# One sum in the output instead of two, a branch at the end of the program and quarter tiles at a later place, in a gated cross-attention and mixture-of-experts kernel

## The chip, the cores and the metric

The kernel runs on one core of a Trainium2 chip. The metric is the device time of one execution in microseconds (us), as the median of several runs; less is better. The engines are PE (TensorE: matmuls and the loads of their weights), DVE (VectorE), ACT (ScalarE), POOL (GpSimd) and SP (SyncE, which here only issues DMAs). Each engine takes its own instructions in order and waits for the others by semaphores.

## The reference

Eight sequences of 256 tokens with 256 features go through a gated cross-attention to 120 context rows (16 heads of 64) and then through a gated mixture of eight experts, two for each token. Cut to what matters:

```python
x = x + tanh(g_xattn) * xattn(layernorm(x), ctx)       # out @ w_out + b_out at its end
def ffn(x, W1, W2, Wr):                                # x: (2048, 256); W1: (8, 1024, 256)
    probs = softmax(einsum('btd,ed->bte', x, Wr))
    vals, idx = top_k(probs, 2)
    gate = sum over the two of  vals / vals.sum(-1) * one_hot(idx, 8)
    h = silu(einsum('btd,efd->btef', x, W1))
    y = einsum('btef,edf->bted', h, W2)
    return einsum('bte,bted->btd', gate, y)
x = x + tanh(g_ffn) * ffn(layernorm(x), W1, W2, Wr)
```

All values are float32.

## The kernel before

**Attention.** A loop over 32 units (sequence, half of the heads, half of the tokens) does the attention. As soon as a sequence is through, its x is the first part of the result; the routing works out each token's two experts, and 32 indirect DMAs of POOL (L366) send each token's normalised row, with its eight gate values and its token number, into the list of each of its experts. The lists lie in a DRAM tensor `routed`. Slots that no token fills hold zeros and a number from 2048 upwards.

**Experts.** The second loop walks a written list `order` of 31 tiles of 128 rows: eight "first" tiles (the first 128 rows of each expert) and the "full" tiles 8 to 30, whose expert is known only at run time. Full tiles 0 to 7 (`SPARE`) and four of the six quads exist for distributions that need more tiles. A "quad" is a tile of four quarters of 32 rows, from up to four experts, for what is left of the lists; two quads (`MIXED`) are worked in halves between the full tiles, so that a quad spreads over four tiles of the list. In iteration i of this loop:

- `go_up` (L837): 32 matmuls with w1 for tile i, then Silu on ACT
- `open_tile`: for tile i+1, DVE copies its expert's w1 (L808) and gate (L813), PE turns its rows (L828), DVE copies them back (L830)
- DVE copies w2 of tile i (L817)
- `close_tile`: 16 matmuls with w2 for tile i-1 (L853), DVE scales the result by the gate into `y` (L861), and `add_up` adds the rows of y to their tokens' rows with an indirect DMA of POOL (L879)
- SP loads the rows of tile i+4 (L796), into one of six buffers (`xt`); the two quads' rows, which POOL gathers (L784), share these buffers

A quad has, in the same iterations, its copies of weights on ACT (L926), its matmuls (L944, L965) and four adds of 32 rows each. There are two buffers for `y`.

**The order of the sums.** Each add waits for the landing of the one before (`last_add`), since two may hit one token's row. There are two places for the sums. The DRAM tensor `acc` has 2048 rows for tokens and 128 more, into which unused slots are added. x is first written into `acc`. The first tiles, the quads and the full tiles 8 to 15 add into `acc`. Then SP copies `acc` to the output `out` (L900), and the last 15 full tiles (`SURE`), which have no unused slots in any case, add into `out`.

**The branch.** Before iteration `always` = 16 a `tc.If(more > 0)` (L1153 in the profile) holds the work of the spare full tiles and of quads 2 to 5. The value `more` is loaded into a register of every engine four iterations earlier. For these inputs it is zero: the branch is passed on all engines, but each has to test it, jump over the body, and bring the semaphores that the body would have raised up to their values. The two quads are mixed into the eight iterations ahead of it.

**Who sets the order.** PE, DVE, ACT and SP keep the order in which the program is written; POOL's instructions are placed by the scheduler. SP is in order too: a load that is written behind the copy of L900 is issued behind it.

Of the kernel before, what the change touches and what calls it, by code (L numbers as in the profile page):

```python
# [9 lines left out]
F32 = mybir.dt.float32  # L10
# [5 lines left out]
P = 128  # L16
# [4 lines left out]
E, DFF = 8, 1024  # L21
# [15 lines left out]
EARLY = 2  # L37
QUARTER = 32
FULLS = 31
SURE = 15  # L40
SPARE = 8
QUADS = 6
MIXED = 2
# [6 lines left out]
def tile_gated_xattn_moe(  # L50
# [36 lines left out]


    routed = tc.dram_tile([E * T + P, XW], F32, name="routed")


    acc = tc.dram_tile([T + P, D], F32, name="acc")

# [295 lines left out]
    ctxT_sb = ap.tile([P, DC, B * M], F32, name="ctxT_sb", bufs=1)  # L391

    x_v = x.rearrange("(n p) d -> p n d", p=P)
    acc_v = acc[:T, :].rearrange("(n p) d -> p n d", p=P)
    ctx_v = ctxT.rearrange("(c p) t -> p c t", p=P)
    wkv_v = w_kv.rearrange("(c p) f -> p c f", p=P)
    wq_v = w_q.rearrange("(c p) f -> p c f", p=P)
# [42 lines left out]
            empty.unsqueeze(1).to_broadcast([P, NBLK, XW]),  # L440
        )
    nc.sync.dma_start(routed[ds(NOWHERE, P), :], empty)
    nc.sync.dma_start(acc[ds(T, P), :], empty[:, :D])

    xns = {}
    norms_x = norms_y = None
# [147 lines left out]
    def norm_y(b, k):  # L594
        nonlocal norms_y
        g = b // 2
        if k == 0:
            if b % 2 == 0:
                groups[g] = [], late.tile([P, DC, GT], F32, tag="xn2T", name=f"xn2T_{g}")
            groups[g][0].append(  # L600
                late.tile([P, 2, XW], F32, tag="rows", name=f"rows_{b}", bufs=4)
            )
            norms_y = Norms(2, f"y{b}")
        norms_y.add(xs[b][:, k, :], groups[g][0][-1][:, k, :D])
        if k == 1:
            nc.sync.dma_start(acc_v[:, ts(b, 2), :], xs[b])
            norms_y.root()

    def turn_y(b, bank):
# [162 lines left out]
    def load(t):  # L772
        kind, i = t
        xt = take(fp, [P, XW], "xt", f"xt_{kind}{i}", bufs=6)
        if kind == "first":
            first = nc.sync.dma_start(xt, routed[ds(i * T, P), :])
            for send in behind:
                tc.declare_no_dep(
                    first.ins, send.ins, reason="rows behind those of the first tiles"
                )  # L780
            firsts.append(first)
            return xt
        if kind == "quad":
            nc.gpsimd.indirect_dma_start(  # L784
                out=xt,
                out_offset=None,
                in_=routed[:, :],
                in_offset=bass.IndirectOffsetOnAxis(
                    ap=tables[1][0][:, i : i + 1], axis=0
                ),  # L790
            )
            return xt
        start = nc.sync.value_load(
            tables[0][1][0:1, i : i + 1], min_val=0, max_val=NOWHERE
        )
        nc.sync.dma_start(xt, routed[ds(start, P), :])  # L796
        return xt
# [52 lines left out]
    def down(t, hT, gate, xt, w2):  # L850
        py = take(fw[2], [P, 512], "mm", f"py_{t[0]}{t[1]}")
        for f in range(FC):
            nc.tensor.matmul(  # L853
                py[:, :D],
                lhsT=hT[:, f, :],
                rhs=w2[:, f, :],
                start=(f == 0),
                stop=(f == FC - 1),
            )
        y = take(fw[3], [P, D], "y", f"y_{t[0]}{t[1]}")  # L860
        nc.vector.tensor_scalar(y, py[:, :D], gate, None, ALU.mult)  # L861
        add_up(t, y, xt)

    def add_up(t, y, xt, parts=1):


        sure = t[0] == "full" and t[1] >= FULLS - SURE
        slots = xt[:, XID : XID + 1].bitcast(I32)
        if parts > 1:

            slots = take(fw[3], [P // parts, parts], "slots", f"slots_{t[1]}", dtype=I32)
            for k in range(parts):
                nc.vector.tensor_copy(
                    slots[:, k : k + 1],
                    xt[ts(k, P // parts), XID : XID + 1].bitcast(I32),
                )
        for k in range(parts):
            own = ts(k, P // parts)
            add = nc.gpsimd.indirect_dma_start(  # L879
                out=out[:, :] if sure else acc[:, :],  # L880
                out_offset=bass.IndirectOffsetOnAxis(
                    ap=slots[:, k : k + 1], axis=0
                ),
                in_=y[own, :],
                in_offset=None,
                compute_op=ALU.add,
            )

            if last_add:
                tc.add_manual_dep(  # L890
                    add.ins,
                    last_add[-1].ins.name,
                    mybir.DependencyInfo(
                        mybir.DependencyClass.Sync, mybir.DependencyReason.DATA
                    ),
                    reason="sums of one token",
                )
            last_add.append(add)
        if t == ("full", FULLS - SURE - 1):
            move = nc.sync.dma_start(out, acc[:T, :])  # L900
            last_add.append(move)


    octets = {}
# [87 lines left out]
    def close_tile():  # L992
        if state["pending"] is not None:
            down(*state["pending"])
            state["pending"] = None
# [5 lines left out]

    order = [("first", e) for e in (0, 1, 2, 6, 3, 4, 5, 7)]
    order += [("full", j) for j in range(SPARE, FULLS)]
    always = E + FULLS - SURE - SPARE
    AHEAD = 4
    xts = {}

# [140 lines left out]
    load_expert(5)  # L1148
    g = NG - 1
    for i, t in enumerate(order):  # L1150
        if i == always:

            with tc.If(more > 0):  # L1153
                spare = {}
                for j in range(SPARE):
                    tj = ("full", j)
                    xt = load(tj)
                    w1, gate, copy_w2 = weights(tj, xt)
                    w2 = copy_w2()
                    down(tj, up(tj, turn(tj, xt), w1), gate, xt, w2)  # L1160
                for j in range(MIXED, QUADS):
                    for _ in quad(j, load(("quad", j))):
                        pass
                spare = None
        if i == always - 4:
            more = nc.values_load(tables[1][3][0:1, 0:1], min_val=0, max_val=FULLS)
        w2_of = state["ready"][2][2]
        if i == 2:
            turn_y(B - 1, bank_tr)


        if i == always - 4 * MIXED - 1:
            quads = [quad(j, xt) for j, xt in enumerate(quad_xts)]
        mixed = i in range(always - 4 * MIXED, always)
        if mixed and i % 4 == 0:
            running = quads[(i - always) // 4 + MIXED]
        if mixed and i != always - 4 * MIXED:
            next(running)
        new = go_up()
        if i == always - 4 * MIXED - 1:  # L1180
            next(quads[0])
        copies = []
        if i == 1:
            for k in range(2):
                copies.append(wide_out(B - 1, k, ps_py))
        if i == 2:
            lg = logits(g, groups[g][1], bank_tr)
            next(lg)
        for k, copy in enumerate(copies):
            copy()  # L1190
            norm_y(B - 1, k)
        if i + 1 < len(order):
            open_tile(order[i + 1], xts[i + 1])
        if mixed:
            next(running)
        if i == 0:
            norms_y.finish()
            weigh(B - 1, 1, ps_py)
            load_expert(4)
            turn_y(B - 2, bank_tr)  # L1200
            sending[g - 1] = places(g - 1, groups[g - 1][0], picked[g - 1], bank_tr)
        if i == 3:
            sending[g] = places(g, groups[g][0], picked[g], bank_tr)
        w2 = w2_of()
        close_tile()
        state["pending"] = *new, w2
        if mixed:
            next(running)
        if i == 1:
            norms_y.finish()  # L1210
        if i == 2:
            lg = next(lg)
            picked[g] = router(g, lg)
        if i < 2:
            for _ in range(2):
                next(sending[g - 1])
        if 2 < i < 5:
            for _ in range(2):
                next(sending[g])
        if i == 4:  # L1220
            parts = table()
            routing_pool.close()
            qp.append(
                ctx.enter_context(
                    tc.tile_pool(name="quads", bufs=1, side="right", reuse_waits="tile")
                )
            )
        if 3 < i < 6:
            tables.append(next(parts))
        while len(xts) <= min(i + AHEAD, len(order) - 1 if tables else 7):  # L1230
            xts[len(xts)] = load(order[len(xts)])
        if i == 5:
            quad_xts = [load(("quad", j)) for j in range(MIXED)]
        if i == 1:
            load_expert(3)
            load_expert(7)
    close_tile()


# [41 lines left out]
```

## Time and profile before

| | |
|---|---|
| median of 3 runs | 556.06 us (555.69 to 557.33) |
| the profiled execution's own time | 555.92 us |
| its span in the profile | 553.8 us |
| PE busy in the span | 529.6 us (96%) |
| weight loads of PE | 448.8 us (81%) |
| DVE, ACT, POOL busy | 285.7, 219.8, 128.3 us |
| mean granted clock of PE | 0.988 |

The span begins with the first instruction and ends with the last; 2.1 us of the execution's time lie outside. A matmul overlaps the next one's weight load, and where PE is busy without gaps it sets the time; the other engines matter where PE, or the last add, waits for them. [...]

### The profile page before, as it was taken

How to read it: one execution, taken by the hardware profiler on the slowest of the kernel's cores; microseconds unless marked ns; L12 is line 12 of the kernel's file. 1: busy time of each engine (PE TensorE's matmuls, PEld its weight loads, DVE VectorE, ACT ScalarE, POOL GpSimd, SP SyncE). 2: the span in 40 equal slices, each digit the busy share in tenths (PEclk: the TensorE clock that was granted, in tenths of full speed). 3: DMA queues.
4: the chain of work that ended last, by engine and by line, in shares of the span. 5: the costliest groups of instructions: out<-in, count | busy, mean ns of one | idle time of the engine just before them, and what ended most of it. 6: DMA issues, size and time to landing. Idle time of an engine off the chain costs nothing. (4 is left out here: it accounts for less than half of the span.)

```text
span 553.8 us, 10097 instructions
## 1 busy us (share of the span) xinstructions
PE 529.6 (96%) x3796; PEld 448.8 (81%) x3796; DVE 285.7 (52%) x683; ACT 219.8 (40%) x700; POOL 128.3 (23%) x135
## 2 busy tenths in 40 slices
PE   7999999999999999999999999999997959999992
PEld 7788878878788787887788989878786959999992
DVE  3676555568655686455742474445343423444430
ACT  1666464564655645556521204455460100111110
POOL 2021100100331003200024463122433423211222
PEclk9999999999999999999999999999999989999997
DMA  8999970500705001020299632222031053222111
GB/s 298 334 308 294 309 219 18 171 22 1 225 35 181 22 1 60 31 69 1 97 381 306 181 89 40 39 30 43 8 51 36 9 181 60 39 40 40 20 19 19
DMA packets 46630, 59.88 MB, mean 108 GB/s; under 512 B 3088, under 2 KB 41616, under 8 KB 46544
## 3 DMA queue, kind: packets, MB, share of 16 engines
q1 hardware_dynamic: 39680, 49.58, 29.3%
q0 software_dynamic: 6480, 8.94, 9.2%
q8 instruction: 32, 0.52, 0.4%
q10 hardware_dynamic: 416, 0.66, 0.4%
q14 instruction: 22, 0.18, 0.1%
HBM read 30.77 MB, written 30.50 MB: 111 GB/s over the span
## 5 line engine op out<-in xcount | busy, mean ns | idle before, releaser
L539 ACT ACTIVATE pr<-psc,mx 128x120 f32<-128x120 f32 x256 | 88.4, 372 | 65.3 <-DVE mx L533 55.9
L837 PEld LDWEIGHTS ph_full<-xT_full,w 128*128 128x128 f32 x736 | 85.2, 192 | 9.2 <-issue 8.5
L837 PE MATMUL ph_full<-xT_full,w 128*128 128x128 f32 x736 | 87.0, 276 | 3.2 <-PEq L1153 2.3
L853 PE MATMUL py_full<-w,hT_full 128*128 128x256 f32 x368 | 84.9, 385 | 0.0
L853 PEld LDWEIGHTS py_full<-w,hT_full 128*128 128x128 f32 x368 | 69.6, 194 | 8.9
L845 ACT ACTIVATE hT_full<-ph_full 128x1024 f32<-128x1024 f32 x23 | 23.5, 1023 | 108.6 <-PE ph_full L837 108.6
L489 PE MATMUL pq<-xnT,w_sb 128*128 128x256 f32 x256 | 62.7, 388 | 0.4 <-DVE xnT L208 0.4
L583 PE MATMUL pw<-w_sb 128*128 128x256 f32 x256 | 58.6, 382 | 0.0
L527 DVE TENSOR_REDUCE mx<-psc 128x8 f32<-128x960 f32 x32 | 37.0, 1156 | 37.5 <-PE psc L519 37.3
L539 ACT ACTIVATION_READ_ACCUMULATOR pr<-psc,mx 128x1 f32 x256 | 55.6, 217 | 0.0
L489 PEld LDWEIGHTS pq<-xnT,w_sb 128*128 128x128 f32 x256 | 46.6, 190 | 10.8 <-issue 3.1
L583 PEld LDWEIGHTS pw<-w_sb 128*128 128x128 f32 x256 | 47.4, 190 | 8.7 <-issue 2.5
L366 POOL DMA_INDIRECT routed<-rows,slot x32 | 31.8, 995 | 56.4 <-DVE slot L362 49.4
L879 POOL DMA_INDIRECT out_dram<-y_full,xt_full x15 | 25.4, 1693 | 77.6 <-DVE y_full L861 57.6
L559 ACT COPY w_sb<-tr 120x512 f32<-120x512 f32 x64 | 34.6, 597 | 19.3 <-PE tr L558 19.3
L548 DVE TENSOR_TENSOR pr<-pr,sm 128x960 f32<-128x960 f32 x32 | 37.1, 1158 | 1.1
L861 DVE TENSOR_SCALAR y_full<-py_full,gate 128x256 f32<-128x256 f32 x23 | 11.1, 484 | 51.1 <-PE py_full L853 44.7
L519 PE MATMUL psc<-kT,w_sb 64*128 64x120 f32 x512 | 37.2, 284 | 0.0
L926 ACT COPY part<-w_sb 128x1024 f32 x32 | 31.1, 1043 | 14.8 <-PE py_q L965 14.2
L519 PEld LDWEIGHTS psc<-kT,w_sb 64*128 64x128 f32 x512 | 31.1, 187 | 6.4 <-issue 3.6
L558 PEld LDWEIGHTS tr<-ident,pr 128*120 128x120 f32 x256 | 29.5, 138 | 5.9 <-issue 4.3
L558 PE MATMUL tr<-ident,pr 128*120 128x128 f32 x256 | 33.5, 273 | 0.1
(175 smaller groups left out, 685.0 us busy)
## 6 DMA issues: line engine op xcount, KB each, us to landing
routed<-w_sb SPq DMA_DIRECT2D x8, 2120.0 KB
w_sb<-in_w1T_dram SPq DMA_DIRECT2D x8, 1024.0 KB
w_sb<-in_w2T_dram SPq DMA_DIRECT2D x8, 1024.0 KB
xt_full<-routed SPq DMA_DIRECT2D x23, 132.5 KB
acc<-x SPq DMA_DIRECT2D x8, 256.0 KB
x<-in_x_dram SPq DMA_DIRECT2D x7, 256.0 KB
w_sb<-in_w_kv_dram SPq DMA_DIRECT2D x3, 512.0 KB
xt_first<-routed SPq DMA_DIRECT2D x8, 132.5 KB
```

Source lines behind the costliest of these rows:

```text
L366: send = nc.gpsimd.indirect_dma_start(out=routed[:, :], out_offset=bass.IndirectOffsetOnAxis(ap=slot[:, i : i + 1], axis=0), in_=rows[h][: ...
L489: nc.tensor.matmul(pq[:, i, :], lhsT=wq_sb[:, c, ts(2 * h + i, P)], rhs=xnT[:, c, :], start=(c == 0), stop=(c == DC - 1),)
L519: nc.tensor.matmul(psc[:, j, ts(i, M)], lhsT=qT[ts(j, DH), 4 * o + i, ts(nb, P)], rhs=kT[ts(j, DH), 4 * o + i, :], start=True, stop=True,)
L527: nc.vector.tensor_reduce(mx.rearrange("p (j i) -> p j i", i=4), psc[:, :, : 4 * M].rearrange("p j (i m) -> p j i m", m=M), AX.X, ALU.max,)
L539: nc.scalar.activation(pr[:, h, :], psc[:, j, ts(i, M)], AF.Exp, bias=mx[:, h : h + 1], scale=QK_SCALE, accum_out=sm[:, h : h + 1],)
L548: nc.vector.tensor_tensor(pr, pr, sm.unsqueeze(2).to_broadcast([P, 8, M]), ALU.mult)
L558: nc.tensor.transpose(tr[:M, i, :], pr[:, 4 * j + i, :], ident)
L559: nc.scalar.copy(pT_sb[:, ts(j, 4), ts(nb, P)], tr[:M, :, :])
L583: nc.tensor.matmul(pw[:, :D], lhsT=oT_sb[b % 2][:, ci, ts(k, P)], rhs=wo_sb[:, ci, :], start=(ci == 0), stop=(ci == IC - 1),)
L837: nc.tensor.matmul(ph[:, f, :], lhsT=w1[:, c, ts(f, P)], rhs=xT[:, c, :], start=(c == 0), stop=(c == DC - 1),)
L853: nc.tensor.matmul(py[:, :D], lhsT=hT[:, f, :], rhs=w2[:, f, :], start=(f == 0), stop=(f == FC - 1),)
L926: nc.scalar.copy(w[:, q, :].rearrange("p (a b) -> p a b", b=D if down else DFF // 2), slab[:, ts(h, FC // 2), :] if down else slab[:, :, t ...
```

## The change

- `acc` is gone. x is written into `out`, and every add goes into `out`. The add gets a bound, the last token's number: a slot with a higher number is left out of the DMA (so the 128 spare rows, their filling, the constant `SURE` and the copy of L900 go too).
- The branch with the spare tiles, and the load of `more`, stand behind the last `close_tile`.
- The two quads are mixed into iterations 16 to 23 instead of 8 to 15. Their gathers are written in iteration 12 instead of 5, and their first copies of weights in iteration 15 instead of 7.

```diff
-SURE = 15
...
-    acc = tc.dram_tile([T + P, D], F32, name="acc")
...
-    acc_v = acc[:T, :].rearrange("(n p) d -> p n d", p=P)
+    out_v = out.rearrange("(n p) d -> p n d", p=P)
...
-    nc.sync.dma_start(acc[ds(T, P), :], empty[:, :D])
...
-            nc.sync.dma_start(acc_v[:, ts(b, 2), :], xs[b])
+            nc.sync.dma_start(out_v[:, ts(b, 2), :], xs[b])
...
-        sure = t[0] == "full" and t[1] >= FULLS - SURE
...
             add = nc.gpsimd.indirect_dma_start(
-                out=out[:, :] if sure else acc[:, :],
+                out=out[:, :],
                 out_offset=bass.IndirectOffsetOnAxis(
                     ap=slots[:, k : k + 1], axis=0
                 ),
                 in_=y[own, :],
                 in_offset=None,
                 compute_op=ALU.add,
+                bounds_check=T - 1,
+                oob_is_err=False,
             )
...
-        if t == ("full", FULLS - SURE - 1):
-            move = nc.sync.dma_start(out, acc[:T, :])
-            last_add.append(move)
...
-    always = E + FULLS - SURE - SPARE
+    mix = 16
...
-        if i == always:
-            with tc.If(more > 0):
-                ...
-        if i == always - 4:
-            more = nc.values_load(tables[1][3][0:1, 0:1], min_val=0, max_val=FULLS)
...
-        if i == always - 4 * MIXED - 1:
+        mixed = mix <= i < mix + 4 * MIXED
+        if i == mix - 1:
             quads = [quad(j, xt) for j, xt in enumerate(quad_xts)]
-        mixed = i in range(always - 4 * MIXED, always)
         if mixed and i % 4 == 0:
-            running = quads[(i - always) // 4 + MIXED]
-        if mixed and i != always - 4 * MIXED:
+            running = quads[(i - mix) // 4]
+        if mixed and i > mix:
             next(running)
         new = go_up()
-        if i == always - 4 * MIXED - 1:
+        if i == mix - 1:
             next(quads[0])
...
-        if i == 5:
+        if i == mix - 4:
             quad_xts = [load(("quad", j)) for j in range(MIXED)]
...
     close_tile()
+
+    more = nc.values_load(tables[1][3][0:1, 0:1], min_val=0, max_val=FULLS)
+    with tc.If(more > 0):
+        spare = {}
+        for j in range(SPARE):
+            tj = ("full", j)
+            xt = load(tj)
+            w1, gate, copy_w2 = weights(tj, xt)
+            w2 = copy_w2()
+            down(tj, up(tj, turn(tj, xt), w1), gate, xt, w2)
+        for j in range(MIXED, QUADS):
+            for _ in quad(j, load(("quad", j))):
+                pass
+        spare = None
```

More of the change, by code (lines that the diff above doesn't have):

```diff
@@ L1150, in tile_gated_xattn_moe @@
     for i, t in enumerate(order):
-        if i == always:
[L1153 to L1164, printed above, removed]
-        if i == always - 4:
-            more = nc.values_load(tables[1][3][0:1, 0:1], min_val=0, max_val=FULLS)
         w2_of = state["ready"][2][2]
```

## The prediction

> **What bounds the kernel now.** I read first the row of busy time and the forty slices of the page: TensorE (PE) is busy for 529.6 of 553.8 us, and its digits fall below 9 almost only near the end. So what PE idles is what can be won. Then I asked for a table by stage of the last part (columns: length, busy time and count of PE, weight load, DVE, ACT, POOL, then granted TensorE clock, DMA share, GB/s):
>
> ```profile
> 339.00:420.00 81.00, 80.89 (x638) 65.41 (x636) 34.79 (x61) 41.54 (x45) 22.05 (x14) 1.00 0.21 34
> 420.00:450.00 30.00, 25.81 (x182) 24.22 (x182) 12.09 (x21) 4.04 (x4) 10.35 (x6) 1.00 0.25 55
> 450.00:462.00 12.00, 7.28 (x32) 6.38 (x33) 2.85 (x5) 0.06 (x1) 3.72 (x2) 0.72 0.44 132
> 462.00:544.00 82.00, 81.55 (x552) 76.24 (x550) 34.94 (x53) 11.27 (x11) 20.14 (x12) 1.00 0.24 35
> 544.00:554.00 10.00, 0.00 (x0) 0.00 (x0) 0.07 (x1) 0.00 (x0) 1.54 (x1) 0.68 0.12 15
> ```
>
> PE is full while the eight mixed tiles run (339 to 420) and in the plain tiles from 462 on. It loses time at 420 to 462, there also with a granted clock of 0.72, and 10 us pass behind its last matmul. The timeline of PE over those holes:
>
> ```profile
> 417.96 1.93 PE L965 MATMUL py_q<-part,hqT 128*32 128x256 f32 x32
> 422.15 2.25 PE L837 MATMUL ph_full<-xT_full,w 128*128 128x128 f32 x18 [2.25 <-PEq L1153]
> 425.38 1.83 PE L837 MATMUL ph_full<-xT_full,w 128*128 128x128 f32 x14 [0.98 <-issue]
> ...
> 434.29 0.38 PE L828 MATMUL xtT_full<-ident,xt_full 128*128 128x128 f32 x2
> ...
> 437.96 3.73 PE L837 MATMUL ph_full<-xT_full,w 128*128 128x128 f32 x32
> ...
> 454.72 0.66 PE L828 MATMUL xtT_full<-ident,xt_full 128*128 128x128 f32 x2 [5.78 <-DMA xt_full<-routed]
> 455.18 5.44 PE L853 MATMUL py_full<-w,hT_full 128*128 128x256 f32 x16
> 460.45 3.73 PE L837 MATMUL ph_full<-xT_full,w 128*128 128x128 f32 x32
> ```
>
> The first hole stands where the branch is (L1153): 2.25 us before the next tile's matmuls, 0.98 us in the middle of them. The second waits for the DMA of a tile's rows. Why was that DMA late? The waits of the DMA queues say it (total us, times, longest):
>
> ```profile
> SPq L900 <- DMA acc<-y_full,xt_full: 21.9, 1, 21.9
> ```
>
> The records of the branch's line, and of the program's last line, give prices used below (minimum/median/maximum ns, first and last start):
>
> ```profile
> L1153 PEldq COMPARE_BRANCH x1: 3542/3542/3542, 418.4 to 418.4; - x1
> ...
> L1153 POOLq COMPARE_BRANCH x1: 53/53/53, 435.8 to 435.8; - x1
> L1153 POOLq INC_SWDGE_SEM x1: 1324/1324/1324, 439.0 to 439.0; - x1
> ```
>
> ```profile
> L1277 POOLq DRAIN x3: 46/113/7812, 545.2 to 553.5; - x3
> ```
>
> And POOL's timeline around the branch:
>
> ```profile
> 418.83 1.54 POOL L879 DMA_INDIRECT acc<-y_full,xt_full  x1 [7.05 <-DVE y_full L861]
> 423.42 1.32 POOL L879 DMA_INDIRECT acc<-half,slots  x1 [3.04 <-DMA acc<-y_full,xt_full]
> ...
> 435.40 2.05 POOL L879 DMA_INDIRECT acc<-half,slots  x1 [2.36 <-DVE xT_full L830]
> 441.19 2.74 POOL L879 DMA_INDIRECT acc<-y_full,xt_full  x1 [3.73 <-DVE y_full L861]
> ```
>
> SP stands 21.9 us at L900, the copy of acc into out, until the last add into acc has landed; tile loads are queued behind it. That add is late because four quarter adds stand before it, each waiting for its predecessor's landing: the chain from 418.83 to 441.19.
>
> **The change part by part.** *The move of acc goes.* No DMA of L900, no 21.9 us wait on SP, no pair of 2 MB streams. The next load, issued at 447.85, is no longer behind it. PE gets back its 5.78 us of idle, and the slow stretch after it: 454.72 to 460.45 is 5.73 us, where the same three groups take 437.96 - 434.29 = 3.67 us, so 2.06 us more. Together **-7.84 us**. Late next is that load's own condition, a free row buffer. Two of the six are held by the quarters; the others come free when an add has landed. For the tile that waits longest (the first one loaded from the buffer of a tile four earlier, with a plain tile between) I take a plain tile's own times: add issued 8.2 us after its tile's up starts, landed 3.7 us later, load about 2.1 us, so the rows are there at 14 us and are turned at 2 x 7.24 + 3.6 = 18.1 us. Some 4 us are left: nothing.
>
> *The branch leaves the middle.* PE gets back 2.25 + 0.98 = **-3.23 us**. DVE's 1.1 us there was under PE's. Without this hole PE comes 3.2 us closer to the add chain. The four quarter adds and the next add follow at 4.0 us on average; DVE's y two tiles later must wait for the add of the tile before (two y buffers). Worked from the rows: that y could start 22.1 us after the quad's last matmul and its add buffer is free at 24.4, so DVE is held 2.3 us. Behind it on DVE stand the copy of w1 (1.23 us), the gate and xT, which PE needs about 2.7 us later than it would get them: no stall, by a thin margin. I book 0, bounds 0 and +0.8 us.
>
> *The quarters move from the 9th to 16th to the 17th to 24th tile.* Their 32 ACT copies of 1.04 us, matmuls, DVE steps and eight adds are the same and lie in the same relation to the neighbouring tiles; a mixed tile took (419.89 - 342.89)/8 = 9.6 us with PE at 80.89 of 81, and takes it there as well. The two gathers on POOL (1.0 us each) leave the place between the last first tiles and go between two adds, where POOL idles 5.7 of 7.24 us; no SP instruction of theirs is moved. At their old place eight plain tiles run, as those after 462. The burst of the second quad is followed by seven plain tiles; an add costs 4.6 us there against 7.24 us a tile, so the backlog of some 12 us is gone in about five of them, before the end. Sum 0.
>
> *The branch goes to the end.* PE's 3.5 us of branch start at 543.5 and end under POOL's last add; DVE, ACT and SP have theirs there too. Exposed is POOL: in the middle its INC_SWDGE_SEM of 1.32 us started at 439.0, once the add of 435.40 had landed. At the end it will start at the landing of the last add, with the final DRAIN behind it and every engine waiting on that. The DRAIN now ends 3.9 us after that landing (549.1 to 553.0), 6.0 us after the add's own end. If it covers the increment, +0; if its tail starts again behind the increment, 549.1 + 1.3 + 6.0 - 553.0 = +3.5. I take the increment alone, **+1.4 us**, since the DRAINs with nothing pending took 0.05 and 0.11 us. [...]
>
> *The bound on every add.* The trace has no bounded indirect DMA. The nearest rows: an add of 128 rows takes 1.54 us to issue, one of 32 rows 1.31, so 2.4 ns a row; doubling that work is +0.3 us. A gain is possible too, as left-out rows are not written, but the last adds are full: lower end 0. I take +0.1 us. On the path are the last two adds only (540.89 and 545.39: the second waits for the first), so **+0.2 us**, bounds 0 and 0.6. [...] The rows give 4.50 us from one chained add to the next, and the chain of 380.3 to 414.1 fills 33.8 of 38.5 us. [...]
>
> The fill of acc's spare rows (128 KB early) lies beside 100 us with PE at 96.8: nothing.
>
> **Sum** against the profiled execution (span 553.8, time 555.92, so 2.1 us around it; the median of the runs, 556.06, is 0.1 above): 553.8 - 7.84 - 3.23 + 1.4 + 0.2 = 544.3, plus 2.1 = **546.4 us**. Ends: 544.8 with nothing at the tail, 549.8 with +3.5, +0.6 and +0.8.
>
> **The rivals.** *Bounded adds are dear* (slower). Sixteen adds stand in the two bursts, and an extra x on each pushes the y writes, DVE's weight copies behind them and then PE. Cover is 4.8 us in the first burst and about 2.5 in the second, and the last two count fully: 18x - 7.3 us. It eats the net gain of 9.5 us at x = 0.93. With x = 1.2, which makes 2.74 us, the dearest add in the trace (441.19), the time is 546.2 + 21.6 - 7.3 = 560.5 us. For it: no row shows such an instruction, and every add gets one. Against: 2.4 ns a row.
>
> [...]
>
> *The move was not the cause.* If the late load waited for its buffer, not for SP, only the branch's 3.2 us goes and 1.6 comes: 554.3, hardly faster. Against: the load follows the copy's issue (446.08) by 1.8 us, with no wait of its own in the list.
>
> **How the numbers follow.** 0.74 for the forecast (544.8 to 549.8), 0.08 for the tail's rival, 0.03 for the move not being the cause, 0.15 for dear adds. About 0.3% (1.7 us) is what a measurement of this kernel can tell from no change; so faster 0.83, same 0.03, slower 0.14. The range, 544.5 to 552.5, holds the forecast and the tail's rival.
>
> **What would show it.** Right: no PE gap over 1 us between 340 us and the last matmul, the granted clock at 1.0 there, the last matmul near 532 us, an INC_SWDGE_SEM of 1.3 us behind the last landing, bounded adds of 1.5 to 1.7 us. Wrong: adds over 2.4 us, PE waiting for DVE's w or y behind the second quad, a row load that PE waits for around the 17th tile, or over 14 us between the last matmul and the end.

## The result, and the profile after

The changed kernel takes 547.8 us (median of four runs, 547.73 to 548.56), the kernel before 556.2 us on the same chip; the ratio is 0.985, with a 95% interval of 0.983 to 0.987. Predicted were 546.4 us with a range of 544.5 to 552.5. The profiled execution took 547.79 us with a span of 546.0.

The table by stage shows where PE's time came back (length, busy time and count of PE, weight load, DVE, ACT, POOL, granted clock, DMA share, GB/s):

```profile
420.00:450.00 30.00, 30.00 (x235) 24.13 (x235) 14.32 (x28) 16.18 (x18) 7.21 (x5) 1.00 0.21 35
450.00:462.00 12.00, 12.00 (x109) 10.38 (x108) 4.51 (x7) 7.50 (x9) 5.31 (x3) 1.00 0.14 14
462.00:534.00 72.00, 69.76 (x488) 62.39 (x485) 29.34 (x48) 13.74 (x15) 26.18 (x15) 1.00 0.24 35
```

Both holes are gone, and the clock stays at 1.00 until the last matmul. The timeline of PE has no idle time worth a mark from 339 us on; its last line is

```profile
524.69 7.07 PE L848 MATMUL py_full<-w,hT_full 128*128 128x256 f32 x32
```

so that PE ends at 531.8 us. In the kernel before it ended at 543.55:

```profile
536.48 7.07 PE L853 MATMUL py_full<-w,hT_full 128*128 128x256 f32 x32
```

That is 11.8 us won, where 11.07 were reckoned. From there to the end of the span it is 14.2 us instead of 10.3: 3.9 us lost, where 1.6 were reckoned. 11.8 - 3.9 is the 7.9 us by which the span is shorter. The records of the branch's line say what the end consists of (minimum/median/maximum ns, first and last start):

```profile
L1217 PEldq COMPARE_BRANCH  x1: 3457/3457/3457, 528.3 to 528.3; - x1
...
L1217 POOLq COMPARE_BRANCH  x1: 53/53/53, 534.0 to 534.0; - x1
L1217 POOLq INC_SWDGE_SEM  x1: 1648/1648/1648, 537.4 to 537.4; - x1
```

The same for the program's last line, the longest of three DRAINs:

```profile
L1268 POOLq DRAIN  x3: 46/107/6036, 539.1 to 545.7; - x3
```

And for the bounded adds of the full tiles:

```profile
L873 POOL DMA_INDIRECT out_dram<-y_full,xt_full x23: 1542/1548/2327, 358.1 to 533.6; - x23
```

POOL's timeline from the second quad's burst to the end:

```profile
481.08 2.18 POOL L873 DMA_INDIRECT out_dram<-half,slots  x1 [2.99 <-DMA out_dram<-y_full,xt_full]
...
516.58 1.55 POOL L873 DMA_INDIRECT out_dram<-y_full,xt_full  x1 [2.98 <-DVE gate L808]
522.08 2.27 POOL L873 DMA_INDIRECT out_dram<-y_full,xt_full  x1 [3.96 <-DVE y_full L856]
529.10 1.55 POOL L873 DMA_INDIRECT out_dram<-y_full,xt_full  x1 [4.75 <-DVE y_full L856]
533.61 1.54 POOL L873 DMA_INDIRECT out_dram<-y_full,xt_full  x1 [2.96 <-DVEq L1217]
```

The last add is issued at 533.61, its row ends at 535.15, and it lands at 537.3; only then the increment runs, to 539.1; only then the DRAIN runs, to 545.1. In the kernel before, POOL's last add was

```profile
545.39 1.54 POOL L879 DMA_INDIRECT out_dram<-y_full,xt_full  x1 [2.95 <-issue]
```

The DRAIN was taken up at 545.2 and took 7.81 us, to 552.97, and the last add ended at 546.93: also 6.04 us from the end of POOL's last work to the end of the DRAIN. But there the last work was the add itself, and its landing, at 549.1, lay inside those 6.04 us.

### The profile page after: what moved, and what is told of

Its sections match the earlier page's. It is cut to its first block, busy times and chain, and to the rows that moved or that the text cites. A ratio compares the mean times of both kernels' runs of the same rounds, so it can differ in the third digit from the quotient of the medians.

```text
span 546.0 us, 10124 instructions
## 1 busy us (share of the span) xinstructions
PE 527.7 (97%) x3796; PEld 448.3 (82%) x3796; DVE 285.8 (52%) x683; ACT 219.5 (40%) x700; POOL 129.3 (24%) x135
## 5 line engine op out<-in xcount | busy, mean ns | idle before, releaser
L848 PE MATMUL py_full<-w,hT_full 128*128 128x256 f32 x368 | 83.1, 379 | 0.0
L848 PEld LDWEIGHTS py_full<-w,hT_full 128*128 128x128 f32 x368 | 68.3, 190 | 8.3
L873 POOL DMA_INDIRECT out_dram<-y_full,xt_full x23 | 39.7, 1726 | 101.0 <-DVE y_full L856 77.7
## 6 DMA issues: line engine op xcount, KB each, us to landing
xt_full<-routed SPq DMA_DIRECT2D x23, 132.5 KB, 2.1
xt_first<-routed SPq DMA_DIRECT2D x8, 132.5 KB, 2.5
```

Of the source, the lines that this page charges most:

```text
L848: nc.tensor.matmul(py[:, :D], lhsT=hT[:, f, :], rhs=w2[:, f, :], start=(f == 0), stop=(f == FC - 1),)
L873: add = nc.gpsimd.indirect_dma_start(out=out[:, :], out_offset=bass.IndirectOffsetOnAxis(ap=slots[:, k : k + 1], axis=0), in_=y[own, :], i ...
```

## The experiments

Theory: the copy of `acc` cost 7.8 us; the branch costs about as much at the end as in the middle, because its increment pushes the DRAIN behind the last landing; the quads' place and the bound cost nothing. Rivals: the branch is the gain; the jump makes the tail; the late quads matter.

### The changed kernel again, and without the branch

The reference of the first group is the changed kernel as it is.

> The changed kernel again, as the reference point of this group: 547.8 us by both theories (547.73 to 548.56 so far).

Measured: 548.3 us (547.82 to 548.69). Then the branch, its body and the load of `more` are left out:

```diff
-    more = nc.values_load(tables[1][3][0:1, 0:1], min_val=0, max_val=FULLS)
-    with tc.If(more > 0):
-        ...
```

> The changed kernel with the branch, its body and the load of more left out (for these inputs the body is never entered). Theory: the end costs 3.95 us, because the increment of POOL's semaphores (1.65 us) starts only after the last add has landed and the final DRAIN then takes its 6.04 us anew, where in the kernel before it lay beside the landing. So 547.8 - 3.95 = 543.9 us, with DRAIN ending 6.0 us after the end of the last add. Rival: the branch at the end is nearly free and the longer tail comes from the bounded add landing later: 547.5 us or more, with the long tail unchanged.

Measured: 543.8 us (543.67 to 543.93), 4.4 us less than the changed kernel in the same group and 4.0 less than its 547.8. The DRAIN's record is back to its old form:

```profile
L1254 POOLq DRAIN  x3: 46/113/7808, 533.6 to 542.0; - x3
```

The last add was issued at 533.83 us and ended at 535.37, and the DRAIN ended at 541.41: 6.04 us later again. From the last matmul to the end it is 10.4 us. So the branch costs all of the longer tail.

### A branch whose body has no adds

`down` gets a switch that leaves out its `add_up`, and the spare quads go from the body:

```diff
     with tc.If(more > 0):
         spare = {}
         for j in range(SPARE):
             ...
-            down(tj, up(tj, turn(tj, xt), w1), gate, xt, w2)
-        for j in range(MIXED, QUADS):
-            for _ in quad(j, load(("quad", j))):
-                pass
+            down(tj, up(tj, turn(tj, xt), w1), gate, xt, w2, False)
```

> The changed kernel with the branch at the end, but with a body from which all of POOL's DMAs are taken out (the adds, and the spare quads with their gathers; for these inputs the body is not entered). PE, DVE, ACT and SP still test and jump. Theory: what costs is the increment of POOL's DMA semaphores and the DRAIN that starts behind it; without adds in the body there is no increment, and the time is that without the branch, 543.8 us (no more than 544.3). [...]

Measured: 544.3 us (543.85 to 544.81), 0.5 us above the kernel without the branch. All engines still test and jump, PE for 3.3 us, and none of that is on the path: from the last matmul to the end it is 10.4 us here too, and PE ends 0.7 us later in this profile, before any branch. There is no increment, and the DRAIN's record shows that it lies beside the landing:

```profile
L1266 POOLq DRAIN  x3: 46/113/7812, 534.4 to 542.8; - x3
```

Had the jump made the tail, the time would have stayed at 547.8 us. So the price of the branch at the end is that of the increment and of what starts behind it.

### One part alone: the sums, and the branch

The first kernel takes the kernel before and changes only the sums:

```diff
-                out=out[:, :] if sure else acc[:, :],
+                out=out[:, :],
...
+                bounds_check=T - 1,
+                oob_is_err=False,
...
-            move = nc.sync.dma_start(out, acc[:T, :])
```

> The kernel before with one part of the change: every add goes into the output with the bound, and the copy of acc is gone; branch and quads stay where they were. Theory: only the stall of the copy goes, 5.78 us of wait and 2.06 us at the halved clock, and the hole of 3.23 us at the branch stays: 556.2 - 7.84 = 548.4 us, so within 1 us of the full change, since moving the branch gives 3.23 us and takes 3.95. Rival: the branch is what the change gains by and the late load would have waited for its buffer anyway: 553 to 556 us, with PE's wait for the tile's rows still at about 449 us.

Measured: 548.3 us (547.92 to 548.55), the same as the full change in the same group, and 7.5 less than the kernel before there (555.8). The wait for the tile's rows is gone; the hole at the branch is left, and in PE's timeline it also cost the clock:

```profile
422.70 5.49 PE L835 MATMUL ph_full<-xT_full,w 128*128 128x128 f32 x32 [2.62 <-PEq L1150]
```

PE waits 2.62 us, and the 32 matmuls behind take 5.49 us instead of 3.84: the granted clock is 0.50 from 423.9 to 427.3 us (0.94 over 420 to 450). The second kernel takes the kernel before and moves only the branch:

```diff
-        if i == always:
-            with tc.If(more > 0):
-                ...
-        if i == always - 4:
-            more = nc.values_load(tables[1][3][0:1, 0:1], min_val=0, max_val=FULLS)
...
     close_tile()
+    more = nc.values_load(tables[1][3][0:1, 0:1], min_val=0, max_val=FULLS)
+    with tc.If(more > 0):
+        ...
```

> The kernel before with the branch moved behind the last tile and nothing else (acc, its copy and the quads' places stay). Theory: PE gets 3.23 us back but then waits about 1.0 us longer for the load behind the copy, as the add chain comes only 2.2 us earlier (the increment of 1.3 us and its wait are gone from it), and the end grows by 3.95 us: 556.2 - 3.23 + 1.0 + 3.95 = 557.9 us, slower. Rival: the branch costs nothing at the end: 553 to 554 us.

Measured: 557.3 us (556.9 to 559.36), slower than the kernel before in the same group: ratio 1.004, interval 1.0025 to 1.0053, which is 1.4 to 3.0 us (the medians lie 1.6 apart). PE, 3.2 us earlier, waits longer for the same late load, by 1.5 us and not by the 1.0 of the expectation. In PE's timeline:

```profile
452.50 0.66 PE L828 MATMUL xtT_full<-ident,xt_full 128*128 128x128 f32 x2 [7.31 <-DMA xt_full<-routed]
```

-3.2 + 1.5 + 3.9 for the tail is +2.2 us. The profile's span grew by 1.6: PE ends 2.3 us earlier, 0.6 more than -3.2 + 1.5, much as it gains 0.7 above the reckoning in the changed kernel. So the whole gain is the copy's; moving the branch alone loses.

### The quads back at their old place

```diff
-    mix = 16
+    mix = 8
...
-        if i == mix - 4:
+        if i == 5:
             quad_xts = [load(("quad", j)) for j in range(MIXED)]
```

> The changed kernel with the two quads back at the 9th to 16th tile (their gathers written in iteration 5 again). Theory: the place of the quads moves work without adding or hiding any: 547.9 us, within 0.5 us of the changed kernel, no gap of PE over 1 us. Rival: the late place is part of the gain, as the second burst of adds is followed by more tiles or by fewer, and PE waits for DVE behind it: off by 1 us or more.

Measured: 547.9 us (547.7 to 548.8), and PE has no gap in its timeline behind 339 us. The place of the quads is worth nothing at the adds' present price.

### Longer links in the chain of adds

No profile shows a dear bounded add, so the rival's working was tried with a step that makes each link longer. It waits for the landing of the add before, and the next add waits for it:

```diff
+            if last_add:
+                pause = nc.gpsimd.tensor_tensor(slow, slow, minus_half[:, :2], ALU.pow)
+                ...
             add = nc.gpsimd.indirect_dma_start(
```

> The changed kernel with an extra step of POOL in every link of the chain of adds: a pow on a 128x2 tile (0.72 us in the trace) that waits for the landing of the add before, and on which the next add waits; about x = 0.9 us for each add with the handing over. It puts the working of the rival 'bounded adds are dear' to the test: 18x - 7.3 = +9 us, so 557 us, with PE waiting for DVE's y or w behind the bursts of quarter adds. If the cover is larger than I reckoned, only the two last adds count: +1.8 us, 549.7 us.

Measured: 554.1 us (550.6 to 555.58; the runs lie in two groups, around 551 and around 555 us, and why is open; the profile is of a run of 554.7). PE lost little, as the one idle mark in its timeline behind 400 us shows,

```profile
508.04 3.84 PE L834 MATMUL ph_full<-xT_full,w 128*128 128x128 f32 x32 [1.25 <-DVE xT_full L827]
```

but from the second quad's burst on POOL does not wait for a `y`; it goes from landing to landing until the last add at 540.44 us, 6.8 us later than in the changed kernel. POOL's timeline from that burst to the end:

```profile
482.04 2.40 POOL L886 DMA_INDIRECT out_dram<-half,slots  x1 [0.29 <-POOL slow L877]
...
525.53 1.59 POOL L886 DMA_INDIRECT out_dram<-y_full,xt_full  x1 [0.29 <-POOL slow L877]
...
530.71 1.59 POOL L886 DMA_INDIRECT out_dram<-y_full,xt_full  x1 [0.29 <-POOL slow L877]
...
535.67 1.59 POOL L886 DMA_INDIRECT out_dram<-y_full,xt_full  x1 [0.29 <-POOL slow L877]
539.43 0.72 POOL L877 TENSOR_TENSOR slow<-slow,minus_half 128x2 f32<-128x2 f32 x1 [2.17 <-DMA out_dram<-y_full,xt_full]
540.44 1.59 POOL L886 DMA_INDIRECT out_dram<-y_full,xt_full  x1 [0.29 <-POOL slow L877]
```

How much longer a link became differs from place to place. The last two take 4.96 and 4.77 us, where a link of the changed kernel that waits for nothing but the landing takes 4.51 at the end: 0.5 at most, as the step partly takes the place of the wait that POOL had behind a landing (2.17 us of idle time ahead of the last step, where 2.96 stood ahead of the last add). But the eight links from the burst's first add to the fifth whole tile behind it take 43.49 us (482.04 to 525.53), where the changed kernel takes 35.50 (481.08 to 516.58): 1.0 us each on average. In the first quad's burst seven links grew by 0.36 each (438.53 to 471.56 against 438.03 to 468.57). With the mean of these fifteen, 0.70 us, my formula gives 18 x 0.70 - 7.3 = +5.3 us; it was +6.2 against 547.9.

So the size is near, but the way is not the formula's, which had the delay reach the end through PE. It came through the chain itself, and the cover that counts is at the chain's end: the changed kernel's chain waits for a `y` only at 522.08 and 529.10, the two adds before the last, where POOL idles 3.96 and 4.75 us instead of the 2.96 that a landing takes. That is 1.0 + 1.8 = 2.8 us of slack. The add that stands at 516.58 in the changed kernel comes 8.95 us later here, and of that the slack takes off 2.8. The same step with the quads early tests this:

> The extra step in every link of the chain of adds again, now with the quads at the 9th to 16th tile. With the quads late, each link grew by only 0.5 us (4.50 to 4.96 us; the step runs partly in the idle time behind a landing), PE waited 1.25 us, and yet the time rose by 6.2 us, as the chain had not caught up by the last tile. Theory: with the quads early fifteen plain tiles follow the second burst, the chain catches up, and only PE's 1.25 us behind the burst and the last link's 0.5 us stay: 547.9 + 1.8 = 549.6 us. Rival: each longer link costs time wherever the bursts lie (DVE held by y, PE behind it): 553 to 555 us, as with the quads late.

Measured: 550.1 us (548.45 to 552.77). With fifteen plain tiles behind the burst the chain catches up (POOL waits for `y` again from 512 us on), and what is left is the last link and PE's wait behind the burst. (The links grew here too, and by more than the 0.5 us of the expectation: the eight behind the second quad's burst by 0.66 each.) In the profile, which is of one of the longer runs (551.0 us of span), that wait is 2.33 us, and the matmuls behind it take 1.6 us more than the usual 3.84:

```profile
451.08 5.46 PE L834 MATMUL ph_full<-xT_full,w 128*128 128x128 f32 x32 [2.33 <-DVE xT_full L827]
```

With 0.42 us for the last link (4.93 instead of the changed kernel's 4.51) that is 4.4 us, and the run lies 4.3 us above the profiled one with the quads early and no step. So the place of the quads does matter, as a reserve that the present adds don't need.

### The branch ahead of the last tile's end

The experiments point to a better place: where POOL's last work is an add again.

```diff
+    more = nc.values_load(tables[1][3][0:1, 0:1], min_val=0, max_val=FULLS)
+    with tc.If(more > 0):
+        ...
     close_tile()
-    more = nc.values_load(...)
-    with tc.If(more > 0):
-        ...
```

> The changed kernel with the branch one step earlier: ahead of the last close_tile, so that POOL's last instruction is an add again and not the increment. Theory: the final DRAIN runs its 6.04 us beside the landing again (-3.95 us); against it PE's last 16 matmuls come 2.3 to 2.6 us late (the branch), and the increment stands between the last two adds, so that the last add is issued 1.8 us later than now. 547.9 - 3.95 + 1.8 = 545.8 us. [...]

Measured: 546.4 us (546.08 to 547.5), 0.6 above the expected 545.8; 0.983 of the kernel before, interval 0.980 to 0.986. PE waits 1.09 us at the branch, the increment lies between the last two adds, the last add is issued at 535.73 us (2.1 later, reckoned 1.8), and the DRAIN overlaps its landing. The record of the increment:

```profile
L1216 POOLq INC_SWDGE_SEM  x1: 1628/1628/1628, 532.9 to 532.9; - x1
```

The DRAIN is taken up just before the last add is issued, as in the kernel before:

```profile
L1268 POOLq DRAIN  x3: 46/112/7812, 535.5 to 543.9; - x3
```

With the quads early as well:

> A candidate for the best version: the branch ahead of the last close_tile and the quads at the 9th to 16th tile. Theory: the two parts do not touch each other: 546.4 us, as with the branch alone moved, as the place of the quads is worth nothing while the chain keeps up. Rival: the increment between the last two adds meets a chain that has only just caught up, and the early quads free it: below 545.9 us.

Measured: 546.3 us (546.22 to 546.4), ratio 0.981, interval 0.980 to 0.983: the two parts do not touch each other, as the theory said. The two medians lie 1.4 and 1.5 us under the changed kernel's 547.8.

## Why the prediction was right, and which of its terms was not

**The move of acc, -7.84 us: right.** The sums alone brought 555.8 to 548.3 in one group, though the hole at the branch cost 1.0 us more there than in the kernel before. The late load did wait behind the copy (issued at 447.85, the copy at 446.08 after 21.9 us of wait on SP), and its own condition, a free row buffer, came in time: PE waits for no rows in the changed kernel. But the wait on SP for the copy's issue, which the prediction put first, is the smaller part of PE's 5.78 us. In the kernel before, the load was issued at

```profile
447.85 0.36 SPq L796 DMA_DIRECT2D xt_full<-routed  x1
```

and its rows were used at 454.7, 6.8 us later. From issue to landing such a load takes in the changed kernel (L791, minimum/median/maximum)

```profile
DMA to landing us min/median/max: 2.0/2.1/3.5
```

The time between is that of the copy's 2 MB (the same columns as above; 362 GB/s for 5.8 us):

```profile
447.40:453.20 5.80, 1.54 (x14) 1.35 (x13) 0.79 (x1) 1.02 (x1) 0.00 (x0) 0.90 0.99 362
```

From 447.0 to 453.2 us the DMA engines moved 32 packets, 2.10 MB together and none under 8 KB; from 453.2 to 455.5 they moved 304 packets under 2 KB, 0.27 MB, which is two tiles' rows of 132.5 KB each. The granted clock was 0.50 from 452.1 to 458.8 us, in which most of PE's slow stretch lies.

My estimate from these rows: issued at 447.85 and landed 2.1 us later, the rows would have cost PE about 1.0 us of idle time, and the copy's bytes cost the other 4.8. The prediction named the pair of 2 MB streams beside the wait on SP, and without the copy both go; no run takes them apart.

**The branch out of the middle, -3.23 us: right.** PE gained 11.8 us in all, 11.07 reckoned; 0.2 of the rest lies in the start of the program (PE's wait for xnT ends at 27.16 instead of 27.36 us). The other 0.4 is how idle time is marked: it counts from the modelled end of a matmul that still overlaps the next, and from start to start the three holes are 2.33, 1.15 and 5.94 us instead of 2.25, 0.98 and 5.78. The thin margin behind the second quad held: no PE gap there.

**The quads, 0: right** (547.9 against 547.8), for the time. That the backlog would be gone "in about five" plain tiles was near: it was gone with the sixth add behind the burst.

**The branch at the end, +1.4 us: the term that was mis-sized.** It was 3.9 us, a little above the upper end of 3.5 that I had worked out. I took the increment alone "since the DRAINs with nothing pending took 0.05 and 0.11 us". That was the wrong neighbour: the nearest row was the DRAIN of before, which ends 6.04 us after the end of POOL's last work, and behind the increment it takes 6.04 us as well. The increment itself is 1.65 us at the end, not 1.32. By the prediction's own sign, "over 14 us between the last matmul and the end", this step was wrong. The upper end of the range, 552.5, and the 0.08 for the tail's rival needed 3.5 us for POOL's branch on top of a DRAIN that starts again; no run shows such a price: POOL's branch took 0.05 us in the middle and at the end, and the kernel with an empty POOL body shows that PE's 3.3 us lie beside other work. What PE's time at the branch consists of, no run here shows.

**The bound, +0.2 us: nothing.** An add of 128 rows takes 1.55 us (median) with it and 1.55 or 1.54 without, and the last two of the chain are 4.51 us apart with it and 4.50 without. So the 4.50 us of the rows held for the chain too.

**Dear adds as a rival:** they did not come. With links made longer the formula's size held roughly (+5.3 against +6.2 us), but by luck: PE, where the formula looked for the delay and its cover (4.8 us in the first burst, about the 38.5 - 33.8 us that the chain left free there), lost 1.25 us, and the rest came at the end of the chain, which has 2.8 us of cover.

The sum was near since the larger terms were read off rows of the trace, and the one term that needed a guess was bounded from both sides; the error is 2.3 us at the end (3.9 against 1.4 + 0.2), less 0.7 that PE gained above the reckoning and 0.3 around the span (1.8 instead of 2.1 us), so 1.3 us of the 1.4. That the 0.7 and the 0.3 lie on the other side is luck.

## What to carry to other kernels

Look at what follows the last instruction of each engine before moving work to the end of a program. Here the increment took 1.32 us in the middle; at the end it took 1.65 us, started only at the last landing and had the DRAIN's 6.04 us behind it, which in the kernel before lay beside a landing: 3.9 us. A copy that waits on an in-order queue costs through what is queued behind it, and here in two ways: the load behind it was issued late, at 447.85 us, after 21.9 us in which SP waited to issue the copy, and then its rows came after the copy's bytes, 5.8 us at 362 GB/s. When a chain of dependent steps has to catch up after a burst, ask how many steps are left before the end, and not only whether the engine it feeds is waiting: the same longer links cost 6.2 us with seven plain tiles behind the burst and 2.2 us with fifteen.

## What the runs showed of the hardware that was not expected

The DRAIN at the end of POOL ended 6.04 us after the end of POOL's last indirect DMA in the profiles of before, without the branch, and with the branch ahead of the last tile; there, and with the empty POOL body, its record is 7.81 us long. Behind the increment, in the profile after, it took 6.04 us. DRAINs behind it, with nothing new on POOL, took 0.05 and 0.11 us. What it waits for is open. The increment (INC_SWDGE_SEM) for the DMAs of a body that is not entered took 1.32 to 1.33 us in the middle of the program and 1.63 to 1.65 us at the end. And a wait of PE of 2.62 us at the branch was followed by 3.4 us at a granted clock of 0.50 in one kernel, and one of 2.33 us, in the kernel with longer links and early quads, by 32 matmuls that took 5.46 us instead of 3.84; while 2.25 us at the branch, with 0.98 more soon behind, were followed by no lower clock in the kernel before (1.00 from 420 to 450). What decides it is open.
